# Diagonals of the weight maxima and the first value projection, moved earlier in a gated cross-attention block

## The chip, the cores and the metric

The kernel runs on one core of one Trainium2 chip. The time is the device time of an execution in microseconds. Three runs of the kernel before gave 665.87, 666.36 and 667.03 us; the median is 666.36 us. A further execution was profiled, and it took 665.6 us.

The engines are called TensorE (PE in the profile, PEld for its weight loads), VectorE (DVE), ScalarE (ACT), GpSimd (POOL) and SyncE (SP, which issues most of the transfers).

## The reference

The block takes `x` (2 x 2048 rows of 512 values) and a context of 77 rows per batch entry, and computes a gated cross-attention followed by a gated feed-forward layer whose operands are rounded to 8-bit steps:

```python
x = x + tanh(g_xattn[0]) * xattn(layernorm(x), ctx, ctx, Wq, bq, Wk, bk, Wv, bv, Wo, bo)
x = x + tanh(g_ffn[0]) * ffn(layernorm(x), w1, b1, w2, b2)

def quant_per_tensor(x):
    scale = max(max(abs(x)), 1e-6) / 127.0
    return round(x / scale), scale

def qlinear(x2d, w, b):
    xq, sx = quant_per_tensor(x2d)
    wq, sw = quant_per_tensor(w)
    return (matmul(xq, wq.T) + b) * (sw * sx)

def ffn(x, w1, b1, w2, b2):
    return qlinear(gelu(qlinear(x, w1, b1)), w2, b2)
```

The attention has 16 heads of 32 values. Each scale is the largest magnitude of a whole tensor, so the largest value of every partition has to be brought together with those of all other partitions.

## The kernel before

The 4096 rows are cut into 8 blocks of 512 rows (index `i`), the 16 heads into 4 groups of 4 (index `g`). The first four blocks belong to the first batch entry, the others to the second. The attention stage runs over the blocks, and in each over 8 steps `s`, two for each head group: each step takes 256 rows of the block.

One step (the loop over `s`, from L456 on) issues work of several ages. `softmax` (L286) computes the scores of the step that comes two steps later: score matmuls on TensorE (L295), the maximum and the subtraction on VectorE (L304, L308), the exponential on ScalarE (L314), the sum and its reciprocal on VectorE (L316, L318), and the product with the reciprocal on GpSimd (L319). `transpose_a` (L325) turns the weights of this step on TensorE (L332), and ScalarE copies them out (L333). `apply_v` (L335) multiplies the turned weights of the head group that is complete with the projected values (L341). `project_o` (L351) makes the output projection of a quarter of the previous block (L354), and VectorE adds it to the residual (L361). `project_q` (L273) projects the queries of a later head group (L276), and ScalarE writes them with their bias (L284). In the last step of a block, `norm2_stats` and `norm2_max` (L365, L370) take the statistics of the second normalization of the previous block and its largest normalized magnitude.

The context is projected once for each batch entry. `project_k` (L215) gives the keys, `project_v` (L235) the values: a matmul group of the weights `wv_sb` with the context (L239, tile pvv), to which VectorE adds the bias rows `bv_sb` (L246, tile vb). For the first batch entry the keys are projected before the loop, and the values in block 0, step 1 (L471, L472), after that step's transposes and in front of the query projection of head group 2. `apply_v` of block 0 needs them from step 2 on.

Weights of the feed-forward layer are quantized beside this. `weight_step` (L411) is called once in each step. In the odd steps of block 1 it takes the largest magnitude of one quarter of w1 for each partition (`weight_max`, L394); in step 0 of block 2 it calls `scale_of` (L166) for w1; in the odd steps of block 2 it quantizes one quarter of w1 after another (L200, L201). Blocks 3 and 4 do the same for w2.

`scale_of` brings the maxima together in one piece: VectorE reduces the quarters to one value for each partition (m_w, L170) and multiplies the identity by it (diag_w, L172), so that the values stand on a diagonal. TensorE multiplies a matrix of ones with this diagonal (pg_w, L174), which gives every partition all 128 values. VectorE takes their maximum (g_w, L176), makes the scale from it (s_w, L178) and its reciprocal (inv_w, L180). The same function serves the activations x (L530) and h (L634) later.

What sets the order: TensorE's order is written out by hand (L432, L451); it executes the matmuls as the program lists them. In front of the loop VectorE's order is by hand as well. From L451 on VectorE's, ScalarE's and GpSimd's queues are laid out by the scheduler, from the order in which the program lists the instructions and from its own estimates of when their inputs are ready; `tc.issue_after` puts an instruction behind a named one. An engine executes its queue in order, so an instruction which waits holds up what stands behind it.

PSUM has three rings of two buffers each. The ring `pp` serves the projections, the applied values, the output projections and the pg_w of `scale_of`; a new tile has to wait until the tile two places earlier has been read.

After block 7 the maximum of x is taken, and the two matmuls of the feed-forward layer follow. They are not touched.

Of the kernel before, what the change touches and what calls it, by code (L numbers as in the profile page):

```python
# [22 lines left out]
NG = HEADS // HG  # L23
# [19 lines left out]
def tile_flamingo_gated_block(  # L43
# [29 lines left out]
    def big(name):  # L73
        return xpool.tile([P, KC, TB], F32, tag="xblk", name=name)
# [11 lines left out]
    def kchunks(w):  # L86
        return w.rearrange("(kc p) n -> p kc n", p=P)
# [63 lines left out]
    xmax = const.tile([P, NB - 1 + NT], F32, name="xmax")  # L151
    hmax = const.tile([P, NB * GT * 2 + 1], F32, name="hmax")
# [10 lines left out]
        nc.gpsimd.tensor_tensor(rstd, ve, mhalf[:, :n], ALU.pow)  # L163
        return last

    def scale_of(maxima, name, psum, tag):  # L166


        m = const.tile([P, 1], F32, name=f"m_{name}")
        nc.vector.tensor_reduce(m, maxima, AX.X, ALU.max)  # L170
        diag = small.tile([P, P], F32, tag="diag", name=f"diag_{name}", bufs=1)
        nc.vector.tensor_scalar(diag, ident, m, None, ALU.mult)  # L172
        pg = psum.tile([P, 512], F32, tag=tag, name=f"pg_{name}")
        nc.tensor.matmul(pg[:, :P], ones, diag, start=True, stop=True)  # L174
        g = const.tile([P, 1], F32, name=f"g_{name}")
        nc.vector.tensor_reduce(g, pg[:, :P], AX.X, ALU.max)  # L176
        s = const.tile([P, 1], F32, name=f"s_{name}")
        nc.vector.tensor_scalar(s, g, MIN_RANGE, 1.0 / QP, ALU.max, ALU.mult)  # L178
        inv = const.tile([P, 1], F32, name=f"inv_{name}")
        nc.vector.reciprocal(inv, s)  # L180
        return s, inv
# [16 lines left out]
    def quantize(dst, src, inv):  # L198

        nc.vector.tensor_scalar(src, src, inv, MAGIC, ALU.mult, ALU.add)  # L200
        return nc.vector.tensor_scalar(dst, src, MAGIC, None, ALU.subtract).ins  # L201
# [4 lines left out]
    s_w, inv_w = {}, {}  # L206
    with actx:
        ps_s = actx.enter_context(tc.tile_pool(name="ps_s", bufs=2, space=PSUM))
        ps_t = actx.enter_context(tc.tile_pool(name="ps_t", bufs=2, space=PSUM))
        ps_p = actx.enter_context(tc.tile_pool(name="ps_p", bufs=2, space=PSUM))  # L210
# [24 lines left out]
        def project_v(b):  # L235

            pv = ps_p.tile([P, 512], F32, tag="pp", name=f"pvv{b}")
            for kc in range(KC):
                nc.tensor.matmul(  # L239
                    pv[:NK, :],  # L240
                    ctx_sb[:, b, kc, :],
                    wv_sb[:, kc, :],
                    start=(kc == 0),
                    stop=(kc == KC - 1),
                )
            nc.vector.tensor_tensor(vblk[b], pv[:NK, :], bv_sb, ALU.add)  # L246
# [26 lines left out]
        def project_q(i, g):  # L273
            pq = ps_p.tile([P, TB], F32, tag="pp", name=f"pq{i}_{g}")
            for kc in range(KC):
                nc.tensor.matmul(  # L276
                    pq,
                    wq_sb[:, kc, g * P : (g + 1) * P],
                    xnT[i][:, kc, :],
                    start=(kc == 0),  # L280
                    stop=(kc == KC - 1),
                )
            qT[i, g] = work.tile([P, TB], F32, tag="qT", name=f"qT{i}_{g}", bufs=5)
            nc.scalar.activation(qT[i, g], pq, AF.Identity, bias=bq_sb[:, g : g + 1])  # L284
# [80 lines left out]
        def norm2_stats(i, t0=0, t1=NT):  # L365
            return layernorm_stats(
                X[i][:, t0:t1, :], mean2[:, i, t0:t1, :], rstd2[:, i, t0:t1], f"f{i}_{t0}"
            )
# [15 lines left out]

        wraw, wmax = {}, {}

        def load_w(name, src, pieces):
            for j in pieces:  # L390
                wraw[name, j] = big(f"raw_{name}{j}")
                nc.sync.dma_start(wraw[name, j], kchunks(src(j)))

        def weight_max(name, j):  # L394
            if j == 0:
                wmax[name] = const.tile([P, 4], F32, name=f"max_{name}")
            nc.vector.tensor_reduce(  # L397
                wmax[name][:, j : j + 1],
                wraw[name, j],
                AX.XY,  # L400
                ALU.max,
                apply_absolute_value=True,
            )
# [7 lines left out]
        def weight_step(i, s):  # L411
            j, odd = divmod(s, 2)
            if i == 1 and odd:
                weight_max("w1", j)
            if i in (2, 4) and s == 0:
                name = "w1" if i == 2 else "w2"
                s_w[name], inv_w[name] = scale_of(wmax[name], name, ps_p, "pp")
            if i == 2 and odd:
                quantize(w1q[:, :, j * TB : (j + 1) * TB], wraw["w1", j], inv_w["w1"])
            if i == 3 and odd:  # L420
                weight_max("w2", j)
                if j < 2:
                    load_w("w2", w2_piece, [j + 2])
                else:
                    load_w("w2", w2_piece, [j - 2])
            if i == 4 and odd:
                quantize(w2q[:, j * KC : (j + 1) * KC, :], wraw["w2", j], inv_w["w2"])
                if j < 2:
                    load_w("w2", w2_piece, [j + 2])
# [22 lines left out]
        softmax(0, 0)  # L452
        softmax(0, 1)
        project_q(0, 1)
        for i in range(NB):
            for s in range(2 * NG):  # L456
                g, odd = divmod(s, 2)
                if not odd and s > 0:
                    apply_v(i, g - 1)
                elif not odd and i > 0:  # L460
                    apply_v(i - 1, NG - 1)
                if s == 5 and i + 1 < NB:
                    for t in (2, 3):
                        transpose_x(i + 1, t)
                if s + 2 < 2 * NG:
                    last = softmax(i, s + 2)
                elif i + 1 < NB:
                    last = softmax(i + 1, s + 2 - 2 * NG)
                for u in range(2):
                    transpose_a(i, s, u)  # L470
                if i == 0 and s == 1:  # L471
                    project_v(0)  # L472
                if i == 0 and s == 2:


                    with tc.issue_after(last["ACT"]):
                        nc.scalar.activation(tg, tg, AF.Tanh)
                    with tc.issue_after(last["POOL"]):
                        nc.gpsimd.tensor_scalar(bo_sb, bo_sb, tg[:, 0:1], None, ALU.mult)
                if not odd and i > 0:  # L480
                    project_o(i - 1, g)
                if s in (1, 3):
                    project_q(i, g + 2)
                elif odd and i + 1 < NB:
                    project_q(i + 1, g - 2)
                if i + 1 < NB:
                    if s == 1:
                        with tc.issue_after(last["DVE"]):
                            norm(i + 1)
                    if s == 3:  # L490
                        for t in (0, 1):
                            transpose_x(i + 1, t)
                if i == 0 and 3 <= s < 7:
                    for b in range(1, B):
                        project_k(b, s - 3)
                        if s == 6:
                            project_v(b)
                if s == 7 and i > 0:
                    norm2_stats(i - 1)
                    norm2_max(i - 1)  # L500
                with tc.issue_after(last["DVE"]):
                    weight_step(i, s)
                    if i == NB - 1 and s == 5:

                        xs0 = work.tile([P, NT, D], F32, tag="aT", name="xs0", bufs=3)
                        for t in range(NT):
                            normalize2(xs0[:, t, :], 0, t)
                t = s - NT if i == 0 else s // 2
                if t >= 0 and (i == 0 or s % 2 == 0):
                    with tc.issue_after(last["POOL"]):  # L510
                        add_bias(i, t)
            if i + 2 < NB:
                load_x(i + 2)
            if i == 0:
                load_w("w1", w1_piece, range(4))
            if i == 2:
                load_w("w2", w2_piece, range(2))
# [9 lines left out]
                    last = norm2_max(NB - 1, t - 1, t)  # L527
        with tc.issue_after(last):
            norm2_max(NB - 1, NT - 1, NT)
        s_x, inv_x = scale_of(xmax, "x", ps_p, "pp")  # L530
        xq0 = work.tile([P, NT, D], BF16, tag="xnT", name="xq0", bufs=1)
        for t in range(NT):
            v, vq = xs0[:, t, :], xq0[:, t, :]
# [29 lines left out]
    ps_g = ctx.enter_context(tc.tile_pool(name="ps_g", bufs=1, space=PSUM, reuse_waits="tile"))  # L563
    with ExitStack() as fctx:
# [27 lines left out]
        for i in range(NB):  # L592
# [4 lines left out]
            for a in range(GT):  # L597
# [32 lines left out]
                else:  # L630
                    stored[i, a] = hidden_dram.tile([P, GF, TB], F32, name=f"h{i}_{a}")
                    nc.sync.dma_start(stored[i, a], G)
    w1ctx.close()
    s_h, inv_h = scale_of(hmax, "h", ps_g, "pg")  # L634
    s2 = const.tile([P, 1], F32, name="s2")


# [113 lines left out]
```

## Time and profile before

| what | value |
|---|---|
| median of the runs | 666.36 us (665.87 to 667.03) |
| profiled execution, its own time | 665.6 us |
| span of its instructions | 663.8 us |
| mean granted TensorE clock | 0.979 |
| TensorE busy | 630.0 us (95%) |
| VectorE busy | 517.9 us (78%) |
| ScalarE busy | 342.9 us (52%) |
| GpSimd busy | 206.2 us (31%) |
| attention stage | from the start to about 424 us |
| DMA, mean | 128 GB/s over the span |

The span is the time from the first to the last instruction of the profiled execution. The page shows it in 40 equal slices of 16.6 us; a digit is the busy share in tenths, and in the line of the clock the granted clock in tenths of full speed. A group of instructions is one line of the program on one engine; `out<-in` names the tile written and the tiles read. In a timeline a row gives start and duration in microseconds, and in brackets the idle time of the engine ahead of it, with the instruction that ended it. Ends of matmuls are modelled. A matmul of 32-bit values shows as two records.

### The profile page before, as it was taken

The numbers are of one execution on the slowest core, as the hardware profiler recorded it, in microseconds if no ns is written. First come the engines' busy times: TensorE is split into PE (matmuls) and PEld (weight loads), VectorE is DVE, ScalarE is ACT, GpSimd is POOL, SyncE is SP. The second block draws the span as 40 slices with busy tenths as digits, with TensorE's granted clock in tenths as the row PEclk, the third lists the DMA queues.
The fourth block names the chain that finished last, engine by engine and source line by source line (L and its number), as shares of the span: only waits on it lengthen the run. The fifth ranks groups of instructions, "written<-read, shape, count | busy, mean of one in ns | idle before, by whom it ended". The sixth has DMA issues, their size and how long they took to land.

```text
span 663.8 us, 8218 instructions
## 1 busy us (share of the span) xinstructions
PE 630.0 (95%) x3048; PEld 320.7 (48%) x3048; DVE 517.9 (78%) x809; ACT 342.9 (52%) x479; POOL 206.2 (31%) x161
## 2 busy tenths in 40 slices
PE   5999999899999899999999999599999979999997
PEld 4565555455455455455554554244444434444443
DVE  3676687887997997986876767999889878887441
ACT  4455444244444344444444442188999879645430
POOL 2234333243333243333333332000000009996000
PEclk9999999799999899999999999799999998999999
DMA  9902100023131113100000000079999208789962
GB/s 280 377 22 88 39 1 0 1 70 121 64 120 72 64 71 120 64 0 1 1 0 1 1 17 1 0 255 329 303 309 345 77 0 326 274 324 357 335 206 79
DMA packets 44255, 84.90 MB, mean 128 GB/s; under 512 B 18795, under 2 KB 22891, under 8 KB 38584
## 3 DMA queue, kind: packets, MB, share of 16 engines
q1 hardware_dynamic: 43112, 83.70, 35.8%
q10 hardware_dynamic: 1104, 0.69, 0.3%
q8 instruction: 24, 0.39, 0.2%
q14 instruction: 15, 0.12, 0.1%
HBM read 49.25 MB, written 31.46 MB: 122 GB/s over the span
## 4 chain that ended last, share of the span: by engine, by line
PE 87%; DVE 10%; ACT 2%; DMA 1%; issue 1%; POOL 0%; ACTq 0%; DVEq 0%
PE pf L668 17%; PE ph L604 17%; PE po L354 15%; PE pq L276 14%; PE pta L332 9%; PE ps L295 6%; PE pc L341 4%; PE ptx L267 2%; DVE tm L376 1%; DVE xf L185 1%; DVE e L308 1%; PE pvv L239 1%; PE pk L219 1%; DVE mx L304 1%; DVE sm L316 1%; DVE max_w L397 1%
## 5 line engine op out<-in xcount | busy, mean ns | idle before, releaser
L319 POOL TENSOR_TENSOR e<-e,rs 128x616 f32<-128x616 f32 x64 | 78.7, 1230 | 231.2 <-DVE rs L318 173.4
L276 PE MATMUL pq<-xnT,wq_sb 128*128 128x512 f32 x256 | 117.3, 602 | 0.8 <-ACT xnT L268 0.8
L668 PE MATMUL pf<-w2q,hq 128*128 128x512 bf16 x512 | 113.6, 386 | 2.3 <-DVE hq L201 2.0
L354 PE MATMUL po<-wo_sb,cT 128*128 128x512 f32 x256 | 114.8, 593 | 0.0
L604 PE MATMUL ph<-xqT,w1q 128*128 128x512 bf16 x512 | 112.1, 382 | 0.7 <-DVE xqT L544 0.7
L333 ACT COPY aT<-pta 77x512 f32<-77x512 f32 x128 | 68.3, 582 | 77.0 <-PE pta L332 76.9
L611 ACT ACTIVATE G<-ph,b1s,s 128x512 f32<-128x512 f32 x128 | 99.5, 778 | 14.1 <-PE ph L604 3.3
L314 ACT ACTIVATE e<-e 128x616 f32<-128x616 f32 x64 | 45.9, 717 | 75.0 <-DVE e L308 73.4
L668 PEld LDWEIGHTS <-hq 128*128 128x128 bf16 x512 | 50.7, 99 | 64.9 <-issue 3.6
L621 DVE TENSOR_REDUCE hmax<-G 128x1 f32<-128x1024 f32 (+1 forms) x65 | 76.6, 1196 | 6.7 <-ACT G L611 6.7
L604 PEld LDWEIGHTS <-w1q 128*128 128x128 bf16 x512 | 50.3, 99 | 62.2 <-issue 1.9
L332 PE MATMUL pta<-ident,e 128*77 128x128 f32 x512 | 72.0, 285 | 0.1
L304 DVE TENSOR_REDUCE mx<-ps 128x8 f32<-128x616 f32 x64 | 50.3, 786 | 27.9 <-PE ps L295 27.4
L276 PEld LDWEIGHTS pq<-xnT,wq_sb 128*128 128x128 f32 x256 | 47.2, 194 | 48.7 <-issue 47.8
L316 DVE TENSOR_REDUCE sm<-e 128x8 f32<-128x616 f32 x64 | 50.6, 790 | 24.7 <-ACT e L314 24.5
L354 PEld LDWEIGHTS po<-wo_sb,cT 128*128 128x128 f32 x256 | 46.4, 190 | 48.2 <-issue 46.6
L332 PEld LDWEIGHTS pta<-ident,e 128*77 128x77 f32 x512 | 57.1, 150 | 11.8 <-issue 10.4
L661 ACT ACTIVATE Gb<-Gb,inv_h 128x2048 f32<-128x2048 f32 x22 | 43.7, 2000 | 36.5 <-DMA Gb<-h 35.5
L295 PEld LDWEIGHTS ps<-kb,qT 64*128 64x128 f32 x512 | 36.4, 188 | 44.9 <-ACT qT L284 22.8
L682 POOL TENSOR_TENSOR x<-x,b_sb 128x512 f32<-128x512 f32 x32 | 56.2, 1793 | 0.1
L308 DVE TENSOR_TENSOR e<-ps,mx 128x616 f32<-128x616 f32 x64 | 51.0, 797 | 2.6
L295 PE MATMUL ps<-kb,qT 64*128 64x154 f32 x512 | 51.3, 320 | 1.6 <-ACT qT L284 1.5
(89 smaller groups left out, 594.7 us busy)
## 6 DMA issues: line engine op xcount, KB each, us to landing
h<-G SPq DMA_DIRECT2D x22, 1024.0 KB, 5.7
Gb<-h SPq DMA_DIRECT2D x22, 1024.0 KB, 7.5
raw_w<-in_w2T SPq DMA_DIRECT2D x8, 1024.0 KB, 5.0
out_y<-x SPq DMA_DIRECT2D x32, 256.0 KB, 2.8
x<-in_x SPq DMA_DIRECT2D x7, 1024.0 KB, 5.3
raw_w<-in_w1T SPq DMA_DIRECT2D x4, 1024.0 KB, 11.7
wk_sb<-in_wkT SPq DMA_DIRECT2D x4, 256.0 KB, 4.9
wq_sb<-in_wqT SPq DMA_DIRECT2D x4, 256.0 KB, 6.1
```

Source lines behind the costliest of these rows:

```text
L276: nc.tensor.matmul(pq, wq_sb[:, kc, g * P : (g + 1) * P], xnT[i][:, kc, :], start=(kc == 0), stop=(kc == KC - 1),)
L295: nc.tensor.matmul(ps[:, q, u * RK : (u + 1) * RK], qT[i, g][r, t * P : (t + 1) * P], kblk[i // NBB][r, g, :], start=True, stop=True,)
L308: last["DVE"] = nc.vector.tensor_tensor(e.rearrange("p u (q r k) -> p q u r k", q=NR, r=RT), sc, mx[:, :, :, :, None].to_broadcast([P, NR, ...
L316: nc.vector.tensor_reduce(sm, e4, AX.X, ALU.add)
L319: last["POOL"] = nc.gpsimd.tensor_tensor(e4, e4, rs[:, :, :, None].to_broadcast([P, 2, HG, NK]), ALU.mult).ins
L332: nc.tensor.transpose(pt[:NK, j, :], es[i, s][:, u, j, :], ident)
L333: nc.scalar.copy(aT[i, g][:, :, t * P : (t + 1) * P], pt[:NK, :, :])
L354: nc.tensor.matmul(po, cT[i, g][:, t * P : (t + 1) * P], wo_sb[:, g, :], start=(g == 0), stop=(g == NG - 1),)
L604: nc.tensor.matmul(ph, w1q[:, kc, fc * P : (fc + 1) * P], cur[:, kc, :], start=(kc == 0), stop=(kc == KC - 1),)
L611: nc.scalar.activation(G[:, 2 * v + u, :], ph, AF.Gelu, bias=b1s[:, fc : fc + 1], scale=s1,)
L621: nc.vector.tensor_reduce(hmax[:, k + u : k + u + 1], G[:, 2 * v + u : 2 * v + u + n, :], AX.XY, ALU.max, apply_absolute_value=True,)
L668: nc.tensor.matmul(po[t], hq[:, fc, t * P : (t + 1) * P], w2q[:, fc, :], start=(fc == 0), stop=(fc == FC - 1),)
```

## The change

`scale_of` is cut in two. A new function `diagonal_of` holds its first two instructions, the reduction to m_w and the product with the identity, diag_w. `scale_of` now takes the diagonal and begins with the matmul.

For w1 and w2 `diagonal_of` is called in `weight_step` in the last step of blocks 1 and 3, right after the maximum of the last quarter. `scale_of` stays in step 0 of blocks 2 and 4. For x and h both functions are called one after the other at the old place.

`project_v(0)` is no longer called in step 1 of block 0 but in front of the loop, after the query projection of head group 1.

```diff
-    def scale_of(maxima, name, psum, tag):
+    def diagonal_of(maxima, name):
         m = const.tile([P, 1], F32, name=f"m_{name}")
         nc.vector.tensor_reduce(m, maxima, AX.X, ALU.max)
         diag = small.tile([P, P], F32, tag="diag", name=f"diag_{name}", bufs=1)
         nc.vector.tensor_scalar(diag, ident, m, None, ALU.mult)
+        return diag
+
+    def scale_of(diag, name, psum, tag):
         pg = psum.tile([P, 512], F32, tag=tag, name=f"pg_{name}")
         nc.tensor.matmul(pg[:, :P], ones, diag, start=True, stop=True)
...
-        wraw, wmax = {}, {}
+        wraw, wmax, wdiag = {}, {}, {}
...
             if i in (2, 4) and s == 0:
                 name = "w1" if i == 2 else "w2"
-                s_w[name], inv_w[name] = scale_of(wmax[name], name, ps_p, "pp")
+                s_w[name], inv_w[name] = scale_of(wdiag[name], name, ps_p, "pp")
...
+            if i in (1, 3) and s == 2 * NG - 1:
+                name = "w1" if i == 1 else "w2"
+                wdiag[name] = diagonal_of(wmax[name], name)
...
         project_q(0, 1)
+        project_v(0)
         for i in range(NB):
...
-                if i == 0 and s == 1:
-                    project_v(0)
...
-        s_x, inv_x = scale_of(xmax, "x", ps_p, "pp")
+        s_x, inv_x = scale_of(diagonal_of(xmax, "x"), "x", ps_p, "pp")
...
-    s_h, inv_h = scale_of(hmax, "h", ps_g, "pg")
+    s_h, inv_h = scale_of(diagonal_of(hmax, "h"), "h", ps_g, "pg")
```

As built, TensorE's queue differs in one place only: pvv stands between pq of head group 1 and ps of step 2, instead of in front of pq of head group 2. VectorE's queue holds the same instructions in another order in three stretches: the add of the bias rows at the start, and the neighbourhoods of pg_w in blocks 2 and 4. The queues of ScalarE, GpSimd and SyncE are the same.

## The prediction

> **What bounds the kernel now.** I read the page first (span, busy time, slices). The profiled execution took 665.6 us, 1.8 us of it outside its span; the median of the runs is 666.36.
>
> ```profile
> span 663.8 us, 8218 instructions
> PE 630.0 (95%) x3048; PEld 320.7 (48%) x3048; DVE 517.9 (78%) x809; ACT 342.9 (52%) x479; POOL 206.2 (31%) x161
> PE   5999999899999899999999999599999979999997
> PEclk9999999799999899999999999799999998999999
> ```
>
> TensorE sets the time, so only what empties TensorE or slows it counts. A slice is 16.6 us; slices 7 and 13 (counting from 0) show 8 on PE and 7 or 8 on the clock. I asked next whom PE waits for:
>
> ```profile
> PE pg_w L174 <- DVE rs L318: 6.1, 2, 3.0
> PE ps L295 <- ACT qT L284: 1.5, 2, 1.3
> ```
>
> These are the waits at the change: two of 3.03 us before pg_w, the matmul that spreads the weights' maxima, and one of 1.32 us before a score matmul. The timeline around the first pg_w (start, duration, idle before in brackets):
>
> ```profile
> 118.67 3.60 PE L354 MATMUL po<-wo_sb,cT 128*128 128x512 f32 x8
> 121.24 0.78 DVE L304 TENSOR_REDUCE mx<-ps 128x8 f32<-128x616 f32 x1
> 121.95 0.67 DVE L376 TENSOR_REDUCE tm<-xf 128x1 f32<-128x512 f32 x1
> 122.55 0.78 DVE L308 TENSOR_TENSOR e<-ps,mx 128x616 f32<-128x616 f32 x1
> 124.88 0.28 DVE L172 TENSOR_SCALAR diag_w<-ident,m_w 128x128 f32<-128x128 f32 x1
> 125.30 0.77 PE L174 MATMUL pg_w<-diag_w,ones 128*128 128x128 f32 x2 [3.03 <-DVE rs L318]
> 133.98 1.06 PE L341 MATMUL pc<-aT,vb 77*32 77x512 f32 x8
> ```
>
> VectorE works without a gap from 110.9 to 125.3, and diag_w stands late in its queue. The three matmul groups between pg_w and pc need 8.68 us here, 7.21 at the second place. Stages show why (columns: length, PE busy, granted clock, DMA):
>
> ```profile
> 122.00:125.00 3.00, 0.27 (x1) 1.00 0.00 0
> 125.00:128.40 3.40, 3.10 (x15) 0.50 0.01 2
> 128.40:131.80 3.40, 3.40 (x9) 0.50 0.00 0
> 224.00:227.40 3.40, 0.93 (x10) 1.00 0.00 0
> 227.40:230.80 3.40, 3.40 (x14) 0.50 0.02 5
> 22.60:26.00 3.40, 2.08 (x7) 1.00 1.06 366
> ```
>
> After each 3.03 us wait the clock is halved, for 6.8 us and for 3.4 us. After the 1.32 us wait it isn't. At the kernel's start:
>
> ```profile
> 20.84 3.70 PE L276 MATMUL pq<-xnT,wq_sb 128*128 128x512 f32 x8
> 25.12 0.69 ACT L284 ACTIVATE qT<-pq,bq_sb 128x512 f32<-128x512 f32 x1
> 25.86 0.80 PE L295 MATMUL ps<-kb,qT 64*128 64x154 f32 x8 [1.32 <-ACT qT L284]
> 29.27 3.60 PE L239 MATMUL pvv<-wv_sb,ctx_sb 128*77 128x512 f32 x8
> ```
>
> The scores of head group 1 wait for ScalarE to evict the query that PE has just projected; pvv, which needs neither, comes 3.4 us later.
>
> **What the Trainium skill says.** "TensorE: Matmul & The Clock Gate", section "What's actually happening": TensorE is at half clock after an idle window of about 3.4 us and at full clock after a busy one; the window (3413 ns) is free-running. The trace has the two clocks and stretches of 6.8 and 3.4 us, but needed no wholly idle window: one with 0.93 us of work was enough, and one with 2.08 us of work was not. The same page, section "Why this matters for your kernels", wants no gap above about 3 us: the 3.03 us gaps dropped the clock, the 1.32 us gap didn't. Its section "Architectural detail" calls ScalarE's and VectorE's queues strict FIFO, which is why diag_w waits its turn here.
>
> **Part 1, the values of batch half 0 before the first step.** Same instructions, moved: pvv (8 matmul records, 3.44 us) now lies between the query's projection and the scores that wait for it. PE can start pvv at about 24.3 and the scores at 27.8; qT ended at 25.81, so that wait is gone. From the start of pq at 20.84 to the start of the first pc at 36.23 are 15.39 us; the groups' start-to-start times without the wait (3.44 + 3.52 + 0.73 + 1.02 + 0.73 + 0.93 + 3.52) make 13.89. Gain 1.3 (the idle time shown) to 1.5; I take 1.4.
> Is pvv ready? Its weights are issued at 8.03 and land 6.7 us later, 14.7; cover of over 9 us. Its bias rows have no landing shown, but the query pieces issued after them on SP's queue at 9.2 to 9.7 land in 7.6 us at most, by 17.3. Its PSUM buffer was last read by ScalarE's copies ending 21.0. No DMA changes place on SP's queue; ScalarE's and POOL's orders are unchanged.
> On VectorE the add of bv now stands in front of the score maximum of group 1, so that maximum slides from 26.70 to about 28.8, and exponentials and normalizing with it (POOL's product from 32.14 to about 34.2). Its transposes come at 37.95 - 1.4 = 36.5: 2.3 us of cover left. What is late next is the normalizing of x1 and score maximum 4 behind it: 38.07 before, about 38.35 now, while PE is 1.4 earlier. Softmax 4 would reach POOL's end near 44.1, wanted at 46.1. Cost nothing; without that cover, up to 0.5 us.
>
> **Part 2, the diagonals of w1 and w2.** Nothing is added; m_w and diag_w move up in VectorE's queue. As built, after the last xf they read m_w, mx, tm, diag_w, xmax, e. With the start-to-start times of before (xf 0.45, m_w 0.07, mx 0.71, tm 0.60, from 120.79) diag_w starts at 122.62 and is done at 122.90 instead of 125.16. PE starts pg_w about 0.1 later, 123.0, where the output projection ended at 122.27: a wait of some 0.75 stays, 2.3 are gone. The second place has the same spacing (xf at 221.96, diag_w at 226.05): again 2.3. Sum 4.6; bounds 3.5 to 5.4, the upper one if diag_w comes half a microsecond sooner.
> So the full "step ahead" isn't gained, since VectorE is behind TensorE there: the remaining 0.75 is VectorE's.
> Behind it: e slides by 0.33, the sum of x and po from 123.38 to 123.6, ended 124.3. The next query projection now waits for that sum by name (its PSUM buffer), and comes at about 125.1: 0.8 us of cover. g_w, s_w and the next maximum follow from 124.4 on, beside PE.
>
> **Part 3, the clock.** At full clock a pg_w costs 0.39 (226.47 to 226.86) and scores, transposes and query projection 5.19 (110.83 to 116.02), together 5.58 up to pc. The excess was 8.68 - 5.58 = 3.1 and 7.21 - 5.58 = 1.6. A 0.75 us wait is shorter than the 1.32 us that left the clock at 1.00, so I take both excesses as gone: 4.7. Bounds: 0 if both drops stay, 4.7.
> Can VectorE follow a PE that is 2.3 plus up to 3.1 us earlier after the first place? By my count the subtraction of scores 4 of this block comes 2.9 us earlier, at 134.4, where PE is 4.5 earlier; POOL's product of it is wanted at 148.0 - 4.5 = 143.5, ready by 139. By the block's end VectorE idles again (0.69, 0.78, 0.94 us at 160 to 165), so nothing is passed on.
>
> **The sum.** 1.4 + 4.6 + 4.7 = 10.7. The profiled execution would go from 665.6 to 654.9, the median from 666.36 to 655.7; between the two I forecast 655.4 us. From about 424 us on, work is only shifted; the clock drops there (waits for pg_x and pg_h) fall elsewhere in the free-running window, worth about 1.7 us each way.
>
> **Rivals.**
> *The clock still drops at one or both places.* For it: the windows where it drops hold light work (scores, transposes) besides the gap. Against: 26.0 to 29.4 is only such work and had 1.00. One drop left costs 1.6 to 3.1, giving 657 to 658.5; both, 655.4 + 4.7 = 660.1.
> *VectorE becomes the bound in blocks 2 and 4.* It is busy 12.0 of 13 us from 141 to 154. If PE stopped for it there, half the gain of part 2 and 3 (4.7) would go: 660. Against: the idle time at 160 to 165.
> *Slower: the bias or value weights land late.* pvv now heads PE's queue, the add heads VectorE's, while the DMA share is at its full 1.06. The gain is eaten when pvv starts 10.7 us late, at 35.0. Loads landing at 14.7 and before 17.3 speak against it; 1 us per us, say 668 if the landing were at 36.
> *The moves don't shift the waits*: diag_w is still released by a later instruction, 665.5 or so. The built order speaks against it.
>
> **Chances.** Forecast (653.5 to 657) 0.68; clock drops stay 0.15; VectorE bound 0.09; slower 0.04; no effect 0.04. The first two and part of the third reach from 653.5 to 660.5, my range; likeliest case alone 653.5 to 657. About 0.2% (1.3 us) is what a measurement of this kernel can tell: faster 0.92, same 0.04, slower 0.04.
>
> **What the changed profile would show.** No wait of PE for qT near 25 us, pvv starting at 24.3, first pc near 34.8. Before each pg_w a wait of 0.5 to 1 us, ended by VectorE. Granted clock 1.00 in both neighbourhoods and 5.6 us from pg_w to pc. I am wrong if a clock drop is still there, if PE waits for x of L361 ahead of the query projection, or for POOL's e ahead of transposes.

## The result and the profile after

| | before | after |
|---|---|---|
| median | 665.87 us (664.34 to 667.03) | 656.11 us (655.05 to 656.76) |
| profiled execution | 665.6 us | 655.2 us |
| its span | 663.8 us | 653.3 us |
| mean granted clock | 0.979 | 0.987 |

The changed kernel needs 0.9855 of the time (95% interval 0.9833 to 0.9877), which is 9.65 us less (8.2 to 11.1); the two medians differ by 9.76 us, and the two profiled executions by 10.4 us.

From the page of the kernel after (busy time and slices; a slice is now 16.3 us):

```profile
span 653.3 us, 8220 instructions
PE 625.0 (96%) x3048; PEld 317.4 (49%) x3048; DVE 514.7 (79%) x809; ACT 342.8 (52%) x479; POOL 204.1 (31%) x161
...
PE   5999999999999999999999999599999979999997
...
PEclk9999999999999999999999999699999989999999
```

Slices 7 and 13 no longer stand out, on PE or on the clock. What is left of low clock lies at the scales of x and h, which the change doesn't touch. TensorE's busy time fell by 5.0 us with the same instructions: that is work done at full instead of half clock.

Whom PE waits for in the kernel after (total us, times, longest us):

```profile
PE pg_w L178 <- DVE diag_w L171: 1.5, 2, 0.7
...
PE pta L336 <- ACT xnT L272: 0.4, 1, 0.4
...
PE ps L299 <- ACT qT L288: 0.2, 1, 0.2
```

The waits before pg_w went from 6.1 us to 1.5, and now name diag_w itself; the score matmul's wait for the query went from 1.5 to 0.2. The line in the middle is new. Around the first pg_w, the timeline of the kernel after:

```profile
117.50 3.60 PE L358 MATMUL po<-wo_sb,cT 128*128 128x512 f32 x8
120.84 0.67 DVE L380 TENSOR_REDUCE tm<-xf 128x1 f32<-128x512 f32 x1
121.43 0.27 DVE L171 TENSOR_SCALAR diag_w<-ident,m_w 128x128 f32<-128x128 f32 x1
121.84 0.46 PE L178 MATMUL pg_w<-diag_w,ones 128*128 128x128 f32 x2 [0.74 <-DVE diag_w L171]
122.39 0.73 DVE L365 SCALAR_TENSOR_TENSOR x<-po,tg,x 128x512 f32<-128x512 f32 x1
123.89 3.60 PE L280 MATMUL pq<-xnT,wq_sb 128*128 128x512 f32 x8
127.42 1.06 PE L345 MATMUL pc<-aT,vb 77*32 77x512 f32 x8
```

diag_w now stands right behind tm in VectorE's queue, and pg_w starts 0.74 us after the output projection has left TensorE idle. From pg_w to pc are 5.58 us, where it was 8.68. The sum of x and po ends at 123.12, and the query projection starts at 123.89 without waiting for it. The windows of the kernel after at both places (length, PE busy, granted clock, DMA share, GB/s):

```profile
121.00:124.00 3.00, 2.26 (x20) 1.00 0.01 3
124.00:127.00 3.00, 3.00 (x9) 1.00 0.00 0
217.00:220.00 3.00, 2.37 (x19) 1.00 0.02 5
220.00:223.00 3.00, 3.00 (x8) 1.00 0.00 0
```

The clock stays at 1.00. The start of the kernel after, timeline:

```profile
24.34 3.60 PE L243 MATMUL pvv<-wv_sb,ctx_sb 128*77 128x512 f32 x8
25.09 0.69 ACT L288 ACTIVATE qT<-pq,bq_sb 128x512 f32<-128x512 f32 x1
27.87 0.80 PE L299 MATMUL ps<-kb,qT 64*128 64x154 f32 x8
34.81 1.07 PE L345 MATMUL pc<-aT,vb 77*32 77x512 f32 x8
44.47 1.06 PE L345 MATMUL pc<-aT,vb 77*32 77x512 f32 x8
50.10 1.07 PE L336 MATMUL pta<-ident,e 128*77 128x128 f32 x8 [0.36 <-ACT xnT L272]
55.38 1.07 PE L345 MATMUL pc<-aT,vb 77*32 77x512 f32 x8
```

The values fill the time in which ScalarE writes qT; the scores follow without a wait. The first pc comes 1.42 us earlier than before (36.23), and so does the second (45.89 before). The third (56.55 before) comes only 1.17 us earlier, because of the new wait at 50.10.

Setting equal places of the two profiled executions side by side gives the account, term by term:

| place | before | after | earlier by | new in this stretch |
|---|---|---|---|---|
| third pc of block 0 | 56.55 | 55.38 | 1.17 | 1.17 values |
| first pg_w | 125.30 | 121.84 | 3.46 | 2.29 wait |
| pc behind it | 133.98 | 127.42 | 6.56 | 3.10 clock |
| second pg_w | 226.47 | 217.63 | 8.84 | 2.28 wait |
| pc behind it | 233.68 | 223.21 | 10.47 | 1.63 clock |

The matmuls pg_x and pg_h, far behind these places, lie 10.46 and 10.48 us earlier than before: from block 4 on nothing is won or given back.

### The profile page after: what moved, and what is told of

It is laid out like the page before. It is cut to its first block, busy times and chain, and to the rows that moved or that the text cites. A ratio compares the mean times of both kernels' runs of the same rounds, so it can differ in the third digit from the quotient of the medians.

```text
span 653.3 us, 8220 instructions
## 1 busy us (share of the span) xinstructions
PE 625.0 (96%) x3048; PEld 317.4 (49%) x3048; DVE 514.7 (79%) x809; ACT 342.8 (52%) x479; POOL 204.1 (31%) x161
## 4 chain that ended last, share of the span: by engine, by line
PE 85%; DVE 11%; ACT 2%; issue 1%; DMA 1%; POOL 0%; ACTq 0%; DVEq 0%
PE pf L674 17%; PE ph L610 17%; PE po L358 15%; PE pq L280 14%; PE pta L336 8%; PE ps L299 6%; PE pc L345 4%; PE ptx L271 2%; DVE tm L380 1%; DVE xf L189 1%; PE pvv L243 1%; DVE mx L308 1%; DVE e L312 1%; DVE sm L320 1%; DVE max_w L401 1%
## 5 line engine op out<-in xcount | busy, mean ns | idle before, releaser
L280 PE MATMUL pq<-xnT,wq_sb 128*128 128x512 f32 x256 | 115.4, 593 | 0.9 <-ACT xnT L272 0.9
L336 PE MATMUL pta<-ident,e 128*77 128x128 f32 x512 | 70.2, 280 | 0.4 <-ACT xnT L272 0.4
L336 PEld LDWEIGHTS pta<-ident,e 128*77 128x77 f32 x512 | 55.6, 147 | 11.8 <-issue 10.3
```

Of the source, the lines that this page charges most:

```text
L280: nc.tensor.matmul(pq, wq_sb[:, kc, g * P : (g + 1) * P], xnT[i][:, kc, :], start=(kc == 0), stop=(kc == KC - 1),)
L336: nc.tensor.transpose(pt[:NK, j, :], es[i, s][:, u, j, :], ident)
```

## The experiments

Every ratio is against runs of the kernel before on the same chip and in the same series; its median was 665.47, 666.19 and 665.35 us in the three series. Times are in microseconds, and a gain is worked out from the ratio unless the medians are named. An unused matmul is one whose result is never read.

### One part alone

**The values alone.** The kernel before, with project_v(0) moved:

```diff
         project_q(0, 1)
+        project_v(0)
         for i in range(NB):
...
-                if i == 0 and s == 1:
-                    project_v(0)
```

> Only the first value projection is moved in front of the first step; the diagonals stay where they were. My sum of parts gives part 1 a gain of 1.3 to 1.5 us at the first pc, of which the changed kernel's trace shows 1.2 left at block 1 (0.25 us went to a wait of transposes for ScalarE near 50 us). So 1.2 us faster than before (664.7 from 665.9), and both clock drops at the weights' scales still there, with waits of 3.0 us before each pg_w. Rival: the two parts are not additive, because the clock window is free-running; then this kernel lies anywhere from 0.5 us slower to 3 us faster, with drops of another length than 6.8 and 3.4 us.

Measured: 665.85 (664.0 to 666.36), ratio 1.0002 (0.9992 to 1.0013). No gain: a miss. The wait for qT is gone as planned, but the timeline of this kernel shows a slower start:

```profile
15.73 5.57 PE L276 MATMUL pq<-xnT,wq_sb 128*128 128x512 f32 x8
23.32 3.70 PE L276 MATMUL pq<-xnT,wq_sb 128*128 128x512 f32 x8
37.32 1.06 PE L341 MATMUL pc<-aT,vb 77*32 77x512 f32 x8
57.91 1.06 PE L341 MATMUL pc<-aT,vb 77*32 77x512 f32 x8
```

The query projection of head group 0 took 5.57 instead of 3.70, and the first pc came 2.5 later than in the kernel after. In this execution TensorE worked at half speed until 19.6, where it got to full speed at 12.3 in the profile of before and at 12.1 in that of after. The moved instructions come after it, so this isn't their doing. Counted from the query projection of head group 1, which leaves the slow start out, the third pc comes after 34.59 (23.32 to 57.91). In the profile of before these are 35.71, and in the other six traces of kernels with the values behind that projection 34.58: the move itself is worth 1.1 in every one of them. The windows of the clock differ as well (same columns as above):

```profile
122.00:125.40 3.40, 1.62 (x4) 1.00 0.00 0
125.40:128.80 3.40, 2.15 (x19) 1.00 0.03 7
221.00:224.40 3.40, 0.70 (x2) 1.00 0.00 0
224.40:227.80 3.40, 3.07 (x15) 0.50 0.02 5
```

The second drop began at 224.40. Counting back 30 windows of 3.413 gives 122.0: here the first gap of 3.03 was cut in two by the edge of a window, both halves held enough work, and the clock did not fall. So one execution of this kernel can win or lose some 2 us by what the edit doesn't touch. More runs of the same kernel:

> The kernel with the value projection alone, once more. If its missing gain was a matter of where the clock windows fell in those runs, it is now 0.5 to 1.5 us faster than before; if the move is worth nothing as long as the clock drops at the weights' scales are there, it is again within 0.5 us of before.

Measured: 664.53 (662.35 to 665.94), ratio 0.9985 (0.9975 to 0.9995): 1.0 less. The two series, 0.0 and -1.0, have intervals that just meet. That slow starts and the positions of the windows blur the 1.1 of the traces is shown for the profiled executions; for the others it is inferred.

**The diagonals alone.** The kernel after, with project_v(0) put back in step 1 of block 0.

> Only the diagonals are issued in the step before; the first value projection stays in step 1. By the sum of parts it keeps 4.6 us of waits and 4.7 us of clock, that is 9.3 us, less what the free-running window gives or takes elsewhere: 656.6 from 665.9. Waits before pg_w of 0.7 to 0.8 us, no clock drop there, the wait of 1.3 us of PE for qT near 25 us back. If the value projection's move had been the larger part (rival), it would be slower than 660.

Measured: 656.75 (656.43 to 657.41), ratio 0.9874 (0.9856 to 0.9891): 8.4 less. The waits before pg_w are 1.5 in all, as in the kernel after, the wait for qT (1.3) is back, and no clock drop is left at pg_w. Most of the gain is this part's, and it doesn't need the other.

### The clock without the diagonals

Three unused matmuls are put ahead of pg_w in the kernel before. They write the tile that pg_w then overwrites; nothing is left out, work is added.

```diff
         pg = psum.tile([P, 512], F32, tag=tag, name=f"pg_{name}")
+        if name in ("w1", "w2"):
+            for _ in range(3):
+                nc.tensor.matmul(pg, ones, wo_sb[:, 0, :], start=True, stop=True)
         nc.tensor.matmul(pg[:, :P], ones, diag, start=True, stop=True)
```

> Kernel of before with three matmuls of ones with a loaded weight (128x512, results never read) ahead of each pg_w. They take 3 x 0.86 = 2.6 us of the 3.03 us that PE waits there; the diagonal comes no earlier. If the clock drops because PE is empty for 3 us, PE starts pg_w at the same time as before, after a wait of 0.45 us, the clock stays at 1.00, and only the clock's part is won: 4.7 us, 661.2 from 665.9. Rival: the drop comes from the light work behind pg_w (scores and transposes); then it is still there, and the time is that of before within 1 us. If the wait alone were the whole cost, also the time of before.

Measured: 661.18 (660.44 to 661.82), ratio 0.9939 (0.9924 to 0.9954): 4.1 less. In the timeline:

```profile
122.06 2.74 PE L176 MATMUL pg_w<-wo_sb,ones 128*128 128x512 f32 x6
125.16 0.49 PE L177 MATMUL pg_w<-diag_w,ones 128*128 128x128 f32 x2 [0.36 <-DVE diag_w L172]
127.24 3.60 PE L279 MATMUL pq<-xnT,wq_sb 128*128 128x512 f32 x8
130.77 1.06 PE L344 MATMUL pc<-aT,vb 77*32 77x512 f32 x8
```

pg_w starts no earlier (125.16; 125.30 before), yet the pc behind it comes 5.61 later instead of 8.68. VectorE's order and its lateness are those of before, so what is won between pg_w and pc is the clock's alone; at the second place these are 5.61 instead of 7.21, together 4.67 in this execution. That settles that the clock drops are a cost of their own, beside the waiting time, and that the scores and transposes behind pg_w, which are still there, don't cause them.

The same with one unused matmul, which leaves an idle time of about 2:

> Kernel of before with one unused matmul ahead of each pg_w, which leaves a wait of 2.2 us. If any wait that leaves the most of a 3.4 us window empty drops the clock, 2.2 us can still do it, by where the window falls: between 0 and 4 us won, and the profile shows a drop at one or none of the two places. If the limit lies at about 3 us of wait, both drops are gone and it is as fast as with three (4.1 us).

Measured: 663.51 (662.55 to 664.85), ratio 0.998 (0.9969 to 0.9992): 1.3 less. Timeline, then windows:

```profile
125.83 0.49 PE L177 MATMUL pg_w<-diag_w,ones 128*128 128x128 f32 x2 [2.07 <-DVE diag_w L172]
128.62 4.57 PE L279 MATMUL pq<-xnT,wq_sb 128*128 128x512 f32 x8
```

```profile
123.70:127.10 3.40, 1.33 (x12) 1.00 0.01 2
127.10:130.60 3.50, 3.50 (x11) 0.51 0.00 0
```

Here a gap of 2.07 still halved the clock for one window of 3.41, at both places. By mean granted clock its runs fall into two groups, 0.981 to 0.982 (664.2 to 664.9) and 0.985 (662.6 to 663.5). The means of the groups lie 1.5 us apart, which fits one drop of 3.41 us at half clock (1.7) that five of the nine are spared; at which place isn't shown, since the profiled one has both drops. The gap of 0.75 in the kernel after cost no clock at either place.

The values and the three unused matmuls together, with the three alone again beside it: a pair in which the drops at pg_w are out of the way.

> The same three unused matmuls, and the first value projection moved. With no clock drop at the weights' scales in either, the move shows its own worth: 1.2 us faster than its partner if the trace is right, nothing if the wait is made up elsewhere.

> The kernel of before with three unused matmuls ahead of each pg_w, once more, as the partner of the next one: again 4.1 us faster than before (between 3 and 5).

Measured: 659.82 (659.12 to 661.08), ratio 0.993 (0.9917 to 0.9942), against 660.7 (660.38 to 661.5), ratio 0.9944 (0.9932 to 0.9957). The values are worth 0.9 here by the medians; the intervals overlap.

**The values in front of the query projection** instead of behind it, in the kernel after:

```diff
         softmax(0, 1)
-        project_q(0, 1)
         project_v(0)
+        project_q(0, 1)
```

> The changed kernel with the value projection one place further ahead, in front of the query projection of head group 1 instead of behind it. If the gain of part 1 comes from filling the wait for qT, and not from moving work to an earlier time, most of it is lost: the scores again follow the projection they wait for, with ScalarE free by then, so a wait of some 0.75 us instead of 1.3 comes back: 0.75 us slower than the changed kernel. Rival (earlier is better): the time of the changed kernel or less.

Measured: 657.01 (655.85 to 659.21), ratio 0.987 (0.985 to 0.989). The waits of PE show what comes back:

```profile
PE ps L299 <- ACT qT L288: 1.0, 2, 0.8
```

Counted from the query projection of head group 0, the third pc is 0.34 earlier than before here, and 1.15 in the kernel after. Early values don't help by being early, but by lying between pq and the scores. The times agree (some 0.9 more than the kernel after) but their intervals overlap; the trace decides this one.

### The remaining 0.75 us before pg_w

The prediction put it down to VectorE's order. First the weights' step was listed ahead of both functions of norm2 in the last step of blocks 1 and 3:

```diff
+                ahead = i in (1, 3) and s == 7
+                if ahead:
+                    with tc.issue_after(last["DVE"]):
+                        weight_step(i, s)
                 if s == 7 and i > 0:
                     norm2_stats(i - 1)
                     norm2_max(i - 1)
                 with tc.issue_after(last["DVE"]):
-                    weight_step(i, s)
+                    if not ahead:
+                        weight_step(i, s)
```

> The changed kernel, with the weights' step in the last step of blocks 1 and 3 issued ahead of the second normalization, so that m_w and diag_w stand before the four xf in VectorE's queue. The remaining wait of 0.75 us before each pg_w is then gone: 1.5 us faster than the changed kernel (654.6 from 656.1), if nothing else is late. Rival: the wait is passed on to the query projection behind pg_w, which waits for VectorE's sum of x and po; that sum ends at 123.1 in the changed kernel, where PE would come at about 123.15; then up to 0.7 us each would show as a wait of pq for x, and the time is that of the changed kernel.

Measured: 657.03 (656.85 to 657.69), ratio 0.9879 (0.9858 to 0.9899): no better than the kernel after. In the waits of PE, the one for diag_w is gone and another has come:

```profile
PE pq L280 <- DVE x L365: 2.8, 2, 1.4
```

Its timeline shows how:

```profile
116.24 0.16 DVE L162 TENSOR_SCALAR ve_f<-mean 128x4 f32<-128x4 f32 x1
...
117.56 1.89 DVE L189 TENSOR_SCALAR xf<-x,mean,rstd 128x512 f32<-128x512 f32 x2 [0.90 <-POOL rstd L163]
...
124.19 0.74 DVE L365 SCALAR_TENSOR_TENSOR x<-po,tg,x 128x512 f32<-128x512 f32 x1
```

The 2.27 us maximum of the weights now stands ahead of ve_f, from which GpSimd makes rstd; so rstd came late, VectorE stood idle for 0.90 us in front of xf, and the sum of x and po started at 124.19 instead of 122.39 (0.5 of this is the later start of this execution). The query projection needs that sum's buffer. The wait was handed on, and grew.

So the weights' step was put between the two functions:

```diff
                 if s == 7 and i > 0:
-                    norm2_stats(i - 1)
+                    stats = norm2_stats(i - 1)
+                    if ahead:
+                        with tc.issue_after(stats):
+                            weight_step(i, s)
                     norm2_max(i - 1)
```

> As the run with the diagonal first, but the weights' step stands behind the statistics of the second normalization instead of ahead of them, so that the variance goes to POOL before the long maximum of the weights. Theory: the 0.9 us for which VectorE waited for POOL's rstd there is gone, the sum of x and po ends where it did in the changed kernel, the diagonal is long there, and PE waits neither before pg_w nor before the query projection: 1.4 us faster than the changed kernel, 654.7 on the scale of its 656.1. Rival: VectorE's chain from the last output projection to the sum of x and po is the bound in any order; then a wait of 0.7 us of pq for x takes the place of the wait of pg_w, and nothing is won.

Measured: 654.34 (654.18 to 654.77), ratio 0.9827 (0.9814 to 0.9841), the best of the kernels without added work. Its timeline:

```profile
116.81 0.24 DVE L171 TENSOR_SCALAR diag_w<-ident,m_w 128x128 f32<-128x128 f32 x1
121.39 0.38 PE L178 MATMUL pg_w<-diag_w,ones 128*128 128x128 f32 x2
122.65 0.74 DVE L365 SCALAR_TENSOR_TENSOR x<-po,tg,x 128x512 f32<-128x512 f32 x1
123.44 3.70 PE L280 MATMUL pq<-xnT,wq_sb 128*128 128x512 f32 x8
```

The diagonal is ready 4.3 us before it is wanted, pg_w follows the output projection without a wait, and the sum of x and po ends at 123.39, 0.05 before pq. That is all the room there is.

### A faster version

The middle order, and unused matmuls wherever TensorE waits long or starts at half clock: 12 of 128 columns at the start, 5 of 512 ahead of pg_x and 2 behind it, 3 ahead of pg_h and 8 of 128 columns behind it.

```diff
+        for _ in range({"x": 5, "h": 3}.get(name, 0)):
+            nc.tensor.matmul(pg, ones, fill, start=True, stop=True)
         nc.tensor.matmul(pg[:, :P], ones, diag, start=True, stop=True)
...
+            idle = ps_p.tile([P, 512], F32, tag="pp", name="idle_0")
+            for _ in range(12):
+                nc.tensor.matmul(idle[:, :P], ones, ones, start=True, stop=True)
```

> The kernel with the diagonal in the middle place, plus matmuls whose results are never read wherever PE is empty for microseconds: 12 of 128x128 at the start, 5 of 128x512 ahead of the pg of x and 2 behind it, 3 ahead of the pg of h and 8 small ones behind it. Theory (the clock follows how empty PE is): full clock from before the first transposes to the end, so the 2.9 us of ph at half clock (1.5 us lost) and the 5.6 us of pf (2.8 us lost) are won, and 1 to 2.5 us at the start: 648 to 650 us. Rival (the clock there follows from something else): 654 to 655.

Measured: 651.14 (651.04 to 652.89), ratio 0.9788 (0.9772 to 0.9803), mean granted clock 1.000 in three of the five runs and 0.997 in two. This beats the kernel before by 14 us and the kernel after by 4 to 5, but falls short of what was expected by 1 us or more. What it gives back is in the trace. At pg_h the unused matmuls outlast the wait that they fill, and g_h waits for PE:

```profile
527.36 2.84 PE L179 MATMUL pg_h<-G,ones 128*128 128x512 f32 x6 [0.87 <-ACT G L635]
528.31 0.28 DVE L171 TENSOR_SCALAR diag_h<-ident,m_h 128x128 f32<-128x128 f32 x1
530.46 0.29 DVE L190 TENSOR_REDUCE g_h<-pg_h 128x1 f32<-128x128 f32 x1 [1.86 <-PE pg_h L180]
```

In the kernel after that wait is 0.58, so 1.3 us went there. Three such matmuls take 2.6 us and TensorE's wait there is 2.2 in the kernel after; what makes them outlast it is in the main the first line: they read the tile G that ScalarE writes last, and so begin 0.87 us late. And a wait of 2.1 us of pf for VectorE's x has come where the kernel after has 0.2; what makes VectorE late there stays open.

The same kernel with project_v(0) back in step 1 of block 0:

> The same with the first value projection back in step 1, where it was before the change. It measures part 1 with no clock drop anywhere in the kernel. If the move is worth what its trace shows and the missing gain of the run with part 1 alone comes from clock windows that fall otherwise, this is 1.2 to 1.5 us slower than the early one. Rival (the move is worth nothing, the wait is made up later): the same time within 0.3 us.

Measured: 652.22 (652.01 to 653.68), ratio 0.9799 (0.9784 to 0.9814). Both profiled executions have no clock drop, and full clock from 4.4 and 5.3 us on. The values' move is worth 1.1 by the medians, 0.7 by the ratios, whose intervals overlap.

## Why the prediction was right, point by point

**The time.** 655.4 was forecast, 656.11 measured, inside the likeliest case's own range (653.5 to 657). The forecast gain was 10.7, the measured one 9.65, with an interval (8.2 to 11.1) that takes in both. Part of the difference is the starting point: the forecast stood on 666.36, the median of three runs, and five runs gave 665.87.

**Part 1, the values.** The mechanism was right: pvv at 24.34 (24.3 forecast), the scores at 27.87 (27.8), the first pc at 34.81 (34.8). The size was too large by about 0.25: the 1.4 are there at the first pc, and 1.13 of them are left at the third (1.17 in the table, with a start that was 0.04 earlier), and as much in every trace with the values behind the query projection. The slide of VectorE in block 0 was costed at nothing, "without that cover, up to 0.5 us"; the cover was thinner than counted. The timeline of the kernel after shows where it went:

```profile
45.57 0.27 DVE L237 TENSOR_SCALAR kb<-pk,bk_sb 32x77 f32<-32x77 f32 x1
45.88 0.32 ACT L235 ACTIVATE kb<-pk,bk_sb 32x77 f32<-32x77 f32 x1 [1.20 <-DVE kb L237]
...
49.37 1.07 ACT L272 COPY xnT<-ptx 128x512 f32<-128x512 f32 x2
```

VectorE's bias of the keys comes 1.08 us earlier than before (46.65), where TensorE is 1.42 earlier. ScalarE's next bias waits for it, and behind that wait ScalarE's queue is only 1.1 to 1.2 earlier; the copy of xnT at its end (50.54 before) lets the transposes wait 0.36 us. The prediction had followed the slide along VectorE and to GpSimd, but not into ScalarE's queue. Over whole runs the pairs of kernels gave 0.7 to 1.1, the part alone 0.0 and 1.0.

**Part 2, the diagonals.** Waits of 0.74 and 0.75 were measured where 0.75 was forecast, and 2.29 and 2.28 us are gone where 2.3 each were forecast. That the rest is VectorE's own lateness was borne out: with diag_w more than four microseconds sooner it vanished. "The Trainium skill", page "TensorE: Matmul & The Clock Gate", section on the architectural detail, calls VectorE's and ScalarE's queues strict FIFO; the experiment with the weights' step in front, where one maximum ahead of ve_f cost a wait of 1.4 us on TensorE, and the 0.36 us wait above, which the bias of the keys hands down ScalarE's queue, agree with it.

**Part 3, the clock.** Full clock at both places, and 5.58 us from pg_w to pc where 5.6 were forecast. In the two profiled executions the gain is the forecast 4.7 (3.10 and 1.63). Over many runs it is less: the unused matmuls alone gave 4.1 and 3.7. This is the term that was mis-sized for the median. It was read from one execution of before, in which the drops lasted 6.8 and 3.4 us. Of the 58 runs of before in the three series, 27 had the mean granted clock of that execution, 0.979; the other 31 had 0.981 or 0.982 and were 1.2 us faster in the mean, as if one drop of 3.41 us were spared. That it is spared at pg_w is likely but not shown: the three profiled executions with 0.981 or 0.982 (the values alone twice, one unused matmul) have 6.8 us of half clock at the two places together, where before has 10.2.

That a wait of 0.75 us is short enough holds by a wide margin: in any window of 3.41 us it leaves 2.66 us for work, and a drop followed only where 1.34 us or less were left (last section).

With 1.0 for the values and 3.9 for the clock from the runs, and the 4.6 of the trace for the waits, the sum is 9.5, against 9.65 measured.

**Two slips in the working.** Behind the first place TensorE was counted as 4.5 us earlier at the transposes of scores 4; the prediction's own 2.3 and 3.1 make 5.4, and so it was measured (5.4, the values' 1.17 left out). It cost nothing, since GpSimd's product was ready at 137.05 and wanted at 141.39. And a landing of the values' loads at 36 gives 667 by the rule stated there, not 668.

**The rivals.** *The clock still drops*: refuted by the windows at both places. *VectorE becomes the bound*: behind pg_w PE has no wait for it in blocks 2 and 4; the query projection that had a forecast cover of 0.8 us has 0.77 (123.12 to 123.89), and the experiment that used up this cover turned it into a wait. It was the next bound, not this one. *Late loads of the values*: pvv started at 24.34 without a wait. *The moves don't shift the waits*: refuted by the waits of PE.

No experiment set the position of the clock's windows, so its share in the scatter of whole runs stays inferred.

## What to carry to other kernels

When an instruction that TensorE waits for has had its inputs for a long time, look for it in the other engine's queue and move it up, behind whatever a third engine waits for and ahead of the rest; a place too far up hands the wait on. Price a gap on TensorE at its length plus what the clock loses behind it, and where the gap can't be closed, a few unused matmuls can keep the clock, if they are fewer than would outlast it and read nothing that is still being written. Take the clock's share from several executions, and follow a slide through every queue that it reaches.

## What the runs showed of the hardware

- Every drop of the granted clock that ended within a kernel lasted a whole multiple of 3.41 us: 3.41 and 6.83 at pg_w in the kernel before, 10.24 around pg_x there, 13.65 at that place with the diagonals alone. The skill's page "TensorE: Matmul & The Clock Gate", section "What's actually happening", has the free-running window of 3413 ns, and the runs agree.
- The length of a gap alone doesn't decide; the work in the window does. All 14 traces, each cut into windows of 3.413 us counted from its own change to full clock, give the same answer: the 31 windows at full clock that a drop followed held 1.34 us of matmuls or less, the 2521 that none followed held 1.49 us or more. So a gap of 2.07 us halved the clock where it fell into one window, and one of 3.03 us didn't where a window's edge parted it into windows with 1.62 and 2.15 us of work. An estimate from these figures: a gap under 1.9 us (3.41 less 1.49) between dense matmuls is safe wherever the window lies. The same page's section "Why this matters for your kernels" asks for no gap above about 3 us; here 2.07 us was already too long, at both places of the profiled execution.
- The cold start, the half clock from the first matmuls on, ended between 12.1 and 19.6 us in the profiled executions of the twelve kernels and repeats that are alike there, and at 4.4 and 5.3 in the two kernels with 12 small unused matmuls at the start. The latest cost 2.5 us up to the first pc. The granted clock of the windows doesn't show it (it reads 1.00 there); the durations of equal matmuls do.
